# Two chunks' values in one PSUM bank, and fixed places for the exponentials, in a two-layer cross-attention block

## The chip, the cores and the metric

The kernel runs on one core of a Trainium2 chip. The metric is device microseconds of one execution. PE is the matrix engine (TensorE; PEld its weight loads), ACT the ScalarE, DVE the VectorE, POOL the GpSimd, SP the engine whose queue issues nearly all DMAs. SBUF is the on-chip memory that all engines read; PSUM, eight banks of 128 partitions by 512 fp32, is what PE writes to.

## What is computed

Two layers, each a self attention, a cross attention and a gated feed-forward part, with layer norms and residuals, for a batch of 4, 512 tokens of width 320, 20 heads of 16, and a context of 1601 rows of width 192:

```python
def _attn(x, ctx, wq, wk, wv, wo, bo, heads):
    q = (x @ wq).reshape(b, n, heads, dh).transpose(0, 2, 1, 3)
    k = (ctx @ wk).reshape(b, j, heads, dh).transpose(0, 2, 1, 3)
    v = (ctx @ wv).reshape(b, j, heads, dh).transpose(0, 2, 1, 3)
    sim = jnp.einsum('bhid,bhjd->bhij', q, k) * dh ** (-0.5)
    a = jax.nn.softmax(sim, axis=-1)
    out = jnp.einsum('bhij,bhjd->bhid', a, v)
    return out.transpose(0, 2, 1, 3).reshape(b, n, heads * dh) @ wo + bo

h1 = _ln(x, n1_g, n1_b)
x = _attn(h1, h1, q1, k1, v1, o1_w, o1_b, heads) + x
h2 = _ln(x, n2_g, n2_b)
x = _attn(h2, context, q2, k2, v2, o2_w, o2_b, heads) + x
h3 = _ln(x, n3_g, n3_b)
a, g = jnp.split(h3 @ ff_w1 + ff_b1, 2, axis=-1)
x = a * jax.nn.gelu(g, approximate=False) @ ff_w2 + ff_b2 + x
```

## The kernel before

**Units.** The work is a list of units, in order: in each layer 20 self units (4 batch entries by 5 groups of 4 heads), 20 cross units (the same) and 4 ff units (one per batch entry). A unit of attention goes through its keys in chunks of 128: 4 chunks in self, 13 in cross (the last has 65 keys). That makes 2 x 20 x (4 + 13) = 680 chunks, 520 of them in cross.

**A chunk** (`main`, L1083). `score` makes the transposed scores of one head, keys on partitions and 512 queries along the free axis, in a bank `st`: two matmuls of the query's high and low parts (`product`, L1096) and one that subtracts the row's maximum (`less_maximum`, L1099). Four heads use the four groups of 32 rows of the PE array, two heads at a time; beside them, in the other two row groups, run the matmuls `sps` (L911) for the maxima of the next unit, which DVE reduces (L932). Then ACT takes the exponential of each `st` into an SBUF tile `pr` (L1109). `values` (L1116) multiplies the values with the four `pr` of a chunk: for each head a matmul to 32 of the 128 partitions of a bank `av` (L1123; two instructions each, so eight a chunk). It is issued one chunk late: `late` collects it and `flush` issues it after the next chunk's scores. The first chunk's `av` is copied to a tile `u.o` (L1134); every further one is copied by ACT to a tile `vo` (L1139) and added to `u.o` by POOL (L1140). In the last cross unit of a layer (`last`) DVE adds the bank to `u.o` instead (L1136), and two of the four `st` lie in `ps_m`.

**The banks.** `ps_st` (L94) has four PSUM banks. The four `st` of a chunk, its `av`, and one bank for most other steps (`step_bank`, L312) are allocated from it, in program order; an allocation waits for the bank that was allocated four before it to be read out. `ps_m` (L95) has two buffers of two banks, for `sps`. The long steps for the context's keys and values (`keys_of_context` L756, `values_of_context` L846) take two banks of `ps_st` and one buffer of `ps_m` (`quarter_banks`, L815).

**The SBUF tiles.** `prs` (L92) is a pool of eight tiles of 128 by 512 fp32, for `pr`, `vo`, and in ff the gate's `gl` and half of the hidden activations `hid` (L1244). `wq1`, `wk1`, `wv1` (L135) hold the self attention's weights, loaded by `load_self` (L191): nine DMAs of rows and six small ones for the norm. `w1` and `w1r` hold the ff weights; in the self and cross stages parts of them hold the cross attention's weights and the context.

**The planner.** Norms, projections (`qps` L702 for queries, `kps` L734 and L764 for keys, `vps` L836 and L854 for values), the output projection (`ops` L1035) and the divisions are steps in chains, each with a cost and a due time counted in rounds, two rounds a chunk. After the `flush` of each chunk `steps` (L372) issues those that are due by a running credit. All of it is decided when the program is built; engines then run their instructions in that order. Steps for the values of a coming unit may only be issued once the unit that uses the place has its values for that chunk (`u.valued`). DMAs of weights wait in a list `loads`; one is issued per chunk, and all that is left at the start of each ff unit (L1439). SP issues DMAs in order.

Of the kernel before, what the change touches and what calls it, by code (L numbers as in the profile page):

```python
# [9 lines left out]
F32 = mybir.dt.float32  # L10
# [7 lines left out]
B, N, D = 4, 512, 320  # L18
S2, CTX = 1601, 192
H, DH = 20, 16  # L20
FF = 4 * D
L = 2
EPS = 1e-5
P = 128
NQ = N // P
G, HG = 5, 4
GD = HG * DH
SLOT = 32
GT = GD // SLOT

VW = DH + 1
# [6 lines left out]
KB = CTX // 32  # L38
# [26 lines left out]
def kernel(ctx: ExitStack, tc: tile.TileContext, x, context, ws, out):  # L65
# [18 lines left out]
    nc = tc.nc  # L84
    dma = nc.sync.dma_start

    const = ctx.enter_context(tc.tile_pool(name="const", bufs=1))
    wpool = ctx.enter_context(tc.tile_pool(name="weights", bufs=1))
    one = ctx.enter_context(tc.tile_pool(name="one", bufs=1))
    two = ctx.enter_context(tc.tile_pool(name="two", bufs=2))  # L90
    three = ctx.enter_context(tc.tile_pool(name="three", bufs=3))
    prs = ctx.enter_context(tc.tile_pool(name="prs", bufs=8))  # L92
    dram = ctx.enter_context(tc.tile_pool(name="dram", bufs=1, space=bass.MemoryType.DRAM))
    ps_st = ctx.enter_context(tc.tile_pool(name="ps_st", bufs=4, space=PSUM))  # L94
    ps_m = ctx.enter_context(tc.tile_pool(name="ps_m", bufs=2, space=PSUM))  # L95
# [6 lines left out]
    columns_of = const.tile([P, NC2 * H * VW + SLOT - VW], F32, name="vals")  # L102
# [29 lines left out]
        return [lambda t=t: part(t) for t in range(NQ)]  # L132


    wq1, wk1, wv1 = (wpool.tile([P, 3, D], F32, name=n) for n in ("wq1", "wk1", "wv1"))  # L135
    wo = wpool.tile([P, 3, D], F32, name="wo")
    w1 = wpool.tile([P, 2, 2 * FF], F32, name="w1")

    w1_flat = w1.rearrange("p k f -> p (k f)")
# [5 lines left out]
    w1r = wpool.tile([P, FF], F32, name="w1r")  # L145
# [4 lines left out]
    wq2 = w2_flat[:, : 3 * D].rearrange("p (k d) -> p k d", d=D)  # L150
    kw = 4 * (HALF + 32)
    kstage = [w2_flat[:, 3 * D + i * kw : 3 * D + (i + 1) * kw].rearrange("p (a w) -> p a w", a=4) for i in range(2)]
    b1 = wpool.tile([P, 2 * NHC], F32, name="b1")

    brow = [wpool.tile([P, D], F32, name=f"brow{i}") for i in range(2)]
# [5 lines left out]
    loads = deque()  # L161
# [29 lines left out]
    def load_self(l):  # L191
        return [lambda: load_norm(l, 0)] + [
            f for t, n in ((wq1, "q1"), (wk1, "k1"), (wv1, "v1")) for f in load_rows(t, ws[l][n], DK)
        ]
# [70 lines left out]
    units = []  # L265
# [44 lines left out]
    start = {"on": True, "both": False}  # L310
# [87 lines left out]
    def until(test, name):  # L398
        while not test():
            assert chains[name], name  # L400
            run(name)
# [113 lines left out]
    def load_context(b, i):  # L515
        c0, n = CGRP[i]
        t = ctx_room[i % 2]
        rows = min(S2, (c0 + n) * P) - c0 * P
        full = rows // P
        if full:  # L520
            dma(
                out=t[:, :full, :],
                in_=context[b, c0 * P : (c0 + full) * P, :].rearrange("(c p) d -> p c d", p=P),
            )
        if rows % P:
            nc.vector.memset(t[rows % P // SLOT * SLOT :, full, :], 0.0)
            dma(out=t[: rows % P, full, :], in_=context[b, (c0 + full) * P : S2, :])
        ctx_in[b, i] = t, clock["round"]
# [537 lines left out]
    late = []  # L1066
# [16 lines left out]
    def main(u, give, nxt):  # L1083

        pr = {}

        def score(c, j, st=None):
            r = min(P, u.nkeys - c * P)
            rows = slice(j * SLOT, (j + 1) * SLOT)
            if st is None:  # L1090
                st = ps_st.tile([P, N], F32, tag="st", name="st")
            keys = u.kT[rows, u.k0 + u.cols[c] : u.k0 + u.cols[c] + r].bitcast(F32R)
            two_rows = slice(j * SLOT, j * SLOT + 2)

            def product(e):
                nc.tensor.matmul(st[:r, :], lhsT=keys, rhs=u.q[rows, e, :].bitcast(F32R), start=(e == 0), stop=False)  # L1096

            def less_maximum():
                nc.tensor.matmul(  # L1099
                    st[:r, :],  # L1100
                    lhsT=units_of[two_rows, :r].bitcast(F32R),
                    rhs=u.mrow[two_rows, :].bitcast(F32R),
                    start=False,
                    stop=True,
                )

            def exponential():
                p = prs.tile([P, N], F32, tag="pr", name="pr")
                nc.scalar.activation(p[:r], st[:r], AF.Exp)  # L1109
                pr[c, j] = p  # L1110

            return [lambda: product(0), lambda: product(1), less_maximum], exponential

        last = nxt is None or nxt.kind == "ff"

        def values(c):  # L1116
            r = min(P, u.nkeys - c * P)
            if u.g in (0, 2):
                until(lambda: units[u.i - u.g].vmade[u.g // 2] > c, "values")
            ps = ps_st.tile([P, N], F32, tag="st", name="av")  # L1120
            for j in range(HG):
                head = (c * H + u.g * HG + j) * VW
                nc.tensor.matmul(  # L1123
                    ps[j * SLOT : (j + 1) * SLOT, :],
                    lhsT=columns_of[:r, head : head + SLOT],
                    rhs=pr.pop((c, j))[:r, :],
                    start=True,
                    stop=True,
                )
            u.valued = c + 1  # L1130

            if c == 0:
                u.o = three.tile([P, N], F32, tag="o", name="o")
                (nc.vector.tensor_copy if last else nc.scalar.copy)(u.o, ps)  # L1134
            elif last:
                nc.vector.tensor_tensor(u.o, ps, u.o, ALU.add)  # L1136
            else:
                vo = prs.tile([P, N], F32, tag="pr", name="vo")
                nc.scalar.copy(vo, ps)  # L1139
                nc.gpsimd.tensor_tensor(u.o, u.o, vo, ALU.add)  # L1140
            if c == u.nch - 1:
                add_finish(u)

        for c in range(u.nch):
            extra = []
            if last:

                both = ps_m.tile([P, 2, N], F32, tag="m", name="st")
                round_of([lambda j=j: score(c, j, both[:, j % 2] if j > 1 else None) for j in range(HG)], [])
                tick()  # L1150
            else:
                for odd in range(2):
                    if odd:
                        tick()
                    pair, rounds = give(2 * c + odd)
                    extra += rounds
                    round_of([lambda j=j: score(c, j) for j in ((2, 3) if odd else (0, 1))], pair)
            u.scored = c + 1

            start["both"] = True  # L1160
            if extra:
                round_of([], extra[0])
            start["both"] = False
            flush()
            late.append(lambda c=c: values(c))
            steps(None, 1 if extra or c == u.nch - 1 else 2)
            for i, e in enumerate(extra[1:]):
                if i and next_cost() is not None:
                    run(pick())
                start["both"] = True  # L1170
                round_of([], e)
                start["both"] = False
            if not last and c == u.nch - 3:
                max_reduce(nxt)
                max_end(nxt)
            if loads:
                loads.popleft()()
# [21 lines left out]
    def ff_main(u, give, nxt):  # L1199
# [42 lines left out]
                    )  # L1242

        def gate(c, pss):  # L1244
            gl = prs.tile([P, N], F32, tag="pr", name="gl")
            nc.scalar.activation(gl, pss[1], AF.Gelu, bias=b1[:, NHC + c : NHC + c + 1])  # L1246
            if c >= len(hid):
                hid.append(prs.tile([P, N], F32, tag="pr", name="hid"))
            nc.vector.scalar_tensor_tensor(hid[c], pss[0], b1[:, c : c + 1], gl, ALU.add, ALU.mult)  # L1249

        def banks():
# [43 lines left out]
    def before(u):  # L1295

        if u.kind == "cross" and u.g == 1 and u.b + 1 < B or u.kind == "self" and u.m == EARLY - 2:
            b = u.b + 1 if u.cross else 0
            if u.l == 0:
                load_context(b, 0)  # L1300
                load_context(b, 1)
        if u.kind == "cross" and u.m == B * G - 1:
            loads.extend(load_first(u.l))
        if u.kind == "self" and u.m == EARLY:

            add_context(u.l, 0, lambda s: units[u.i - u.m + B * G].own.update(kv=s["cT"], tail=s["tail"]), u.start + 36, yes)

    def after(u):

        stage[u.b] += 1  # L1310
        if u.b == B - 1:
            load_bias(u.l, ("self", "cross", "ff").index(u.kind) + 2)
            if u.kind == "self":
                loads.extend(load_out(u.l, "o2_w"))
            if u.kind == "cross" and u.l + 1 < L:
                loads.extend(load_out(u.l + 1, "o1_w"))
            if u.l + 1 < L:
                if u.kind == "ff":
                    loads.extend(load_cross(u.l + 1))
                    loads.extend(load_ff(u.l + 1))  # L1320
                elif u.kind == "self":
                    loads.extend(load_self(u.l + 1))

    def left(v):
        return sum(map(len, v.pairs))
# [152 lines left out]
```

## Time and profile before

| what | value |
| --- | --- |
| median of 3 runs | 3263.91 us (3244.82 to 3268.62) |
| profiled execution, time | 3260.33 us |
| profiled execution, span | 3258.5 us |
| mean granted clock of PE | 0.965 of full |
| exponentials `pr` (L1109), ACT | 2720, 603 ns each |
| copies `vo` (L1139), ACT | 576, 606 ns each |
| adds `o` (L1140), POOL | 576, 1284 ns each |
| values `av` (L1123), PE | 5440 instructions, 765.4 us busy in all |
| maxima `pm` (L932), DVE | 980, 1194 ns each |

In the stages, the self attention of layer 0 ends and its cross attention begins at 456 us of the span; the cross attention goes to about 1368, the ff to about 1666, the second layer's self attention to 2065 and its cross attention to about 2978. The page gives busy times per engine, the chain of work that ended last, and groups of instructions by line. Busy times of PE are of pipelined matmuls whose ends are modelled, so that a short wait can lie inside a busy stretch. The list of waits names, for each engine and line, what ended an idle time: microseconds in total, how often, and the longest. The timeline gives instructions in order of time: start and length in us, engine, line, operation, what is written from what, and in brackets the idle time before. `PEld` is a weight load, and a bank that a matmul must wait for is waited for by its weight load already.

### The profile page before, as it was taken

Reading aid. Unit: us, or ns where it says so; the run is one execution under the profiler, and the core shown is the slowest. Engines: PE = TensorE matmul, PEld = TensorE weight load, DVE = VectorE, ACT = ScalarE, POOL = GpSimd, SP = SyncE. Lnnn points to the kernel's source line nnn. Section 1 sums busy time; section 2 is a strip of 40 time slices with the busy share of each in tenths; the row PEclk is TensorE's granted clock in tenths of the full one; section 3 lists DMA queues with packets and bytes.
Section 4 is the critical chain, followed back from the end, with each engine's and each line's share of the span. In section 5 each row is a group of like instructions: output and inputs, shape, how many; then the busy total and the mean of one; then the engine's idle time right before and its main releaser. Section 6 shows DMA issues by size and latency. Waiting matters only on the chain.

```text
span 3258.5 us, 87733 instructions
## 1 busy us (share of the span) xinstructions
PE 3075.1 (94%) x36690; PEld 1632.1 (50%) x36690; DVE 2097.2 (64%) x2845; ACT 1961.6 (60%) x3949; POOL 1263.3 (39%) x1369
## 2 busy tenths in 40 slices
PE   7899899999999999999998998999999999999999
PEld 3455455455455455455444554554554555544555
DVE  6766777777777777622256777777777777774221
ACT  2666556787777777711136664677777778776110
POOL 2435334554544544211114453345445445442000
PEclk7999889999999999999999998999999999999999
DMA  3333212211211211200113231212121111112000
GB/s 91 86 68 79 44 37 53 66 38 39 54 39 40 63 31 36 69 1 5 26 32 74 66 65 38 43 41 53 33 50 39 36 41 39 40 22 65 9 11 14
DMA packets 213029, 145.00 MB, mean 44 GB/s; under 512 B 65556, under 2 KB 203160, under 8 KB 212632
## 3 DMA queue, kind: packets, MB, share of 16 engines
q1 hardware_dynamic: 211368, 138.32, 19.1%
q8 instruction: 289, 4.73, 0.6%
q10 hardware_dynamic: 1264, 1.06, 0.1%
q14 instruction: 108, 0.88, 0.1%
HBM read 33.04 MB, written 7.93 MB: 13 GB/s over the span
## 4 chain that ended last, share of the span: by engine, by line
PE 69%; DVE 11%; POOL 5%; ACT 4%; issue 4%; SPq 3%; DMA 3%; ACTq 0%; DVEq 0%; POOLq 0%
PE av L1123 16%; PE st L1096 14%; PE fps L1223 9%; PE yps L1279 5%; PE st L1099 5%; DVE pm L932 4%; PE sps L911 4%; ACT pr L1109 4%; PE kps L764 3%; PE vps L854 3%; PE qps L702 3%; PE ops L1035 3%; PE fps L1236 2%; DVE nmax L932 2%; SPq L991 2%
## 5 line engine op out<-in xcount | busy, mean ns | idle before, releaser
L1109 ACT ACTIVATE pr<-st 128x512 f32<-128x512 f32 (+1 forms) x2720 | 1414.0, 603 | 422.0 <-PE st L1099 362.9
L932 DVE TENSOR_REDUCE pm<-sps 128x2 f32<-128x1024 f32 (+1 forms) x980 | 1132.8, 1194 | 197.6 <-PE sps L911 155.8
L1140 POOL TENSOR_TENSOR o<-o,vo 128x512 f32<-128x512 f32 x576 | 739.8, 1284 | 1194.8 <-ACT vo L1139 1145.4
L1096 PE MATMUL st<-q,kT 32*128 32x512 f32 (+1 forms) x5440 | 1021.2, 444 | 50.6 <-ACT pr L1109 19.2
L911 PE MATMUL sps<-kT,q 32*128 32x512 f32 (+1 forms) x6400 | 988.7, 410 | 55.2 <-DMA kT<-stage 24.0
L1123 PE MATMUL av<-pr,vals 128*32 128x512 f32 (+1 forms) x5440 | 765.4, 630 | 35.5 <-ACT pr L1109 32.8
L1096 PEld LDWEIGHTS st<-q,kT 32*128 32x128 f32 (+1 forms) x5440 | 505.0, 183 | 517.3 <-ACT pr L1109 283.1
L1099 PE MATMUL st<-m,units 2*128 2x512 f32 (+1 forms) x2720 | 620.4, 401 | 20.0 <-DMA m<-turned 18.0
L911 PEld LDWEIGHTS sps<-kT,q 32*128 32x128 f32 x6400 | 478.7, 188 | 105.6 <-DVE pm L932 33.7
L932 DVE TENSOR_REDUCE nmax<-sps 128x2 f32<-128x1024 f32 (+1 forms) x356 | 381.3, 1110 | 174.8 <-PE sps L911 120.1
L1139 ACT COPY vo<-av 128x512 f32<-128x512 f32 x576 | 348.8, 606 | 52.5 <-PE av L1123 50.2
L1099 PEld LDWEIGHTS st<-m,units 2*128 2x128 f32 (+1 forms) x2720 | 317.3, 184 | 67.2 <-issue 27.1
L1223 PE MATMUL fps<-hT,w 128*128 128x512 f32 x640 | 284.6, 597 | 1.8 <-DVE hid L1249 1.8
L1246 ACT ACTIVATE gl<-fps,b 128x512 f32<-128x512 f32 x80 | 50.6, 684 | 369.7 <-PE fps L1236 268.1
L1123 PEld LDWEIGHTS av<-pr,vals 128*32 128x32 f32 (+1 forms) x5440 | 111.7, 109 | 303.9 <-ACT pr L1109 282.1
L1249 DVE SCALAR_TENSOR_TENSOR hid<-fps,b,gl 128x512 f32<-128x512 f32 x80 | 56.4, 747 | 252.5 <-ACT gl L1246 252.5
L1223 PEld LDWEIGHTS fps<-hT,w 128*128 128x128 f32 x640 | 118.6, 190 | 151.2 <-issue 145.9
L609 POOL TENSOR_SCALAR stage<-stage 128x256 fp32r<-128x256 f32 (+1 forms) x155 | 107.2, 692 | 183.9 <-ACT stage L710 97.8
L1279 PE MATMUL yps<-w,hid 128*128 128x320 f32 x640 | 175.4, 434 | 0.0
L1279 PEld LDWEIGHTS yps<-w,hid 128*128 128x128 f32 x640 | 120.6, 190 | 55.8 <-issue 7.0
L609 POOL TENSOR_SCALAR w<-w 128x896 fp32r<-128x896 f32 x40 | 98.1, 2452 | 109.1 <-DVE w L774 109.1
L1035 PEld LDWEIGHTS ops<-wo,aT 112*32 112x32 f32 (+1 forms) x3072 | 100.5, 113 | 67.4 <-issue 34.0
(82 smaller groups left out, 2310.5 us busy)
## 6 DMA issues: line engine op xcount, KB each, us to landing
kT<-w SPq DMA_DIRECT2D x160, 192.0 KB
q<-stage SPq DMA_DIRECT2D x320, 64.0 KB
q<-stage SPq DMA_DIRECT2D x154, 128.0 KB
aT<-o SPq DMA_DIRECT2D x320, 32.0 KB
m<-turned SPq DMA_DIRECT2D x636, 2.0 KB
kT<-stage SPq DMA_DIRECT2D x156, 64.0 KB
w<-in_L_xattn_ff_w_dram SPq DMA_DIRECT2D x20, 256.0 KB
ctxT<-ctxT SPq DMA_DIRECT2D x24, 208.0 KB
```

The lines of the kernel that those rows point to most:

```text
L609: eng.tensor_scalar(high.bitcast(F32R), x, 1.0, None, ALU.mult)
L911: nc.tensor.matmul(out, lhsT=u.q[rows, e, queries].bitcast(F32R), rhs=u.kT[rows, keys].bitcast(F32R), start=(e == 0), stop=(e == 1),)
L932: nc.vector.tensor_reduce(to[:, j : j + n], part, AX.X, ALU.max, negate=(ns == 1))
L1035: nc.tensor.matmul(ps[f : f + m, : D // 2], lhsT=aT[:n, k, t * P + f : t * P + f + m], rhs=wo[:n, k, cols], start=(k == 0), stop=(k == 2),)
L1096: nc.tensor.matmul(st[:r, :], lhsT=keys, rhs=u.q[rows, e, :].bitcast(F32R), start=(e == 0), stop=False)
L1099: nc.tensor.matmul(st[:r, :], lhsT=units_of[two_rows, :r].bitcast(F32R), rhs=u.mrow[two_rows, :].bitcast(F32R), start=False, stop=True,)
L1109: nc.scalar.activation(p[:r], st[:r], AF.Exp)
L1123: nc.tensor.matmul(ps[j * SLOT : (j + 1) * SLOT, :], lhsT=columns_of[:r, head : head + SLOT], rhs=pr.pop((c, j))[:r, :], start=True, stop= ...
L1139: nc.scalar.copy(vo, ps)
L1140: nc.gpsimd.tensor_tensor(u.o, u.o, vo, ALU.add)
L1223: nc.tensor.matmul(ps, lhsT=w1[:, k, i * FF + c * P : i * FF + (c + 1) * P], rhs=u.hT[:, k, :], start=ahead and k == 0, stop=not ahead and ...
L1279: nc.tensor.matmul(ps[:, :D], lhsT=hid[c][:, t * P : (t + 1) * P], rhs=w2[:, c, :], start=(c == 0), stop=(c == NHC - 1),)
```

## The change

Three things are changed together. In cross units `values` takes a list of two chunks: the matmuls of both go to one bank, the first chunk's with `start`, the second's with `stop`, so that PE adds them up; then one copy and one add follow for the two. It is issued one chunk after the second, so in the program even chunks (2, 4, ... 12) are followed by 16 value instructions and odd ones by none; the thirteenth chunk stands alone and is issued in the next unit's first chunk. Self units go on with one chunk at a time.

The pool `prs` is replaced by a fixed tile `own` of eight places, and `place()` goes round them in turn: in self units ten places (two more in unused columns of `w1` and `w1r`), in cross units thirteen (five more in the self attention's weights, which become one tile `wself`). The ff part uses the eight places by number.

Because cross now writes to the self attention's weights, `load_self` for the next layer is put into `loads` at the first ff unit, and no longer at the end of the self stage.

```diff
-    prs = ctx.enter_context(tc.tile_pool(name="prs", bufs=8))
...
-    wq1, wk1, wv1 = (wpool.tile([P, 3, D], F32, name=n) for n in ("wq1", "wk1", "wv1"))
+    wself = wpool.tile([P, 9 * D], F32, name="wself")
+    wq1, wk1, wv1 = (wself[:, i * 3 * D : (i + 1) * 3 * D].rearrange("p (k d) -> p k d", d=D) for i in range(3))
...
+    own = const.tile([P, 8, N], F32, name="pr")
+    mine = [own[:, i, :] for i in range(8)]
+    places = {
+        "self": mine + [w1_flat[:, (2 * KB + 2) * D : (2 * KB + 2) * D + N], w1r[:, 4 * CTX : 4 * CTX + N]],
+        "cross": mine + [wself[:, i * N : (i + 1) * N] for i in range(5)],
+    }
+    at_place = {"kind": "self", "i": -1}
+
+    def place():
+        these = places[at_place["kind"]]
+        at_place["i"] = (at_place["i"] + 1) % len(these)
+        return these[at_place["i"]]
...
+        if at_place["kind"] != u.kind:
+            at_place.update(kind=u.kind, i=min(at_place["i"], len(mine) - 1))
...
-                p = prs.tile([P, N], F32, tag="pr", name="pr")
+                p = place()
...
-        def values(c):
-            r = min(P, u.nkeys - c * P)
+        def values(cs):
             if u.g in (0, 2):
-                until(lambda: units[u.i - u.g].vmade[u.g // 2] > c, "values")
+                until(lambda: units[u.i - u.g].vmade[u.g // 2] > cs[-1], "values")
             ps = ps_st.tile([P, N], F32, tag="st", name="av")
-            for j in range(HG):
-                head = (c * H + u.g * HG + j) * VW
-                nc.tensor.matmul(
-                    ps[j * SLOT : (j + 1) * SLOT, :],
-                    lhsT=columns_of[:r, head : head + SLOT],
-                    rhs=pr.pop((c, j))[:r, :],
-                    start=True,
-                    stop=True,
-                )
-            u.valued = c + 1
-
-            if c == 0:
+            for c in cs:
+                r = min(P, u.nkeys - c * P)
+                for j in range(HG):
+                    head = (c * H + u.g * HG + j) * VW
+                    nc.tensor.matmul(
+                        ps[j * SLOT : (j + 1) * SLOT, :],
+                        lhsT=columns_of[:r, head : head + SLOT],
+                        rhs=pr.pop((c, j))[:r, :],
+                        start=(c == cs[0]),
+                        stop=(c == cs[-1]),
+                    )
+            u.valued = cs[-1] + 1
+
+            if cs[0] == 0:
...
-                vo = prs.tile([P, N], F32, tag="pr", name="vo")
+                vo = place()
...
-            if c == u.nch - 1:
+            if u.valued == u.nch:
                 add_finish(u)
+
+
+        n = 2 if u.cross else 1
+        together = {min(c + n, u.nch) - 1: list(range(c, min(c + n, u.nch))) for c in range(0, u.nch, n)}
...
-            late.append(lambda c=c: values(c))
+            if c in together:
+                late.append(lambda cs=together[c]: values(cs))
...
-            gl = prs.tile([P, N], F32, tag="pr", name="gl")
+            gl = mine[5 + c % 3]
...
-                hid.append(prs.tile([P, N], F32, tag="pr", name="hid"))
+                hid.append(mine[c - 5])
...
+        if u.kind == "ff" and u.b == 0 and u.l + 1 < L:
+            loads.extend(load_self(u.l + 1))
...
-                elif u.kind == "self":
-                    loads.extend(load_self(u.l + 1))
```

## The prediction

> **What bounds the kernel now.** I read the page first, for the busy shares and the chain that ended last.
>
> ```profile
> PE 3075.1 (94%) x36690; PEld 1632.1 (50%) x36690; DVE 2097.2 (64%) x2845; ACT 1961.6 (60%) x3949; POOL 1263.3 (39%) x1369
> ...
> PE 69%; DVE 11%; POOL 5%; ACT 4%; issue 4%; SPq 3%; DMA 3%; ACTq 0%; DVEq 0%; POOLq 0%
> ```
>
> PE carries the chain; ACT and POOL, which the change relieves, hold 4% and 5% of it. So ACT or POOL time that goes is worth only what PE waits for. The list of waits, longest first, says where that is.
>
> ```profile
> ACT pr L1109 <- PE st L1099: 362.9, 517, 11.7
> ...
> PEld st L1096 <- ACT pr L1109: 283.1, 349, 1.7
> PEld av L1123 <- ACT pr L1109: 282.1, 610, 0.7
> ...
> ACT pr L1109 <- POOL o L1140: 37.3, 27, 1.6
> ```
>
> `PEld av <- ACT pr` is no wait for data, since the values read exponentials a chunk old. It is the wait for a PSUM bank: the four banks of `ps_st` hold a chunk's four `st`, and the next allocation, `av`, needs the first of them back from its exponential. 610 of 680 chunks have it. Next, the timeline of two neighbouring cross chunks (start, length):
>
> ```profile
> 1315.99 0.16 PEld L1123 LDWEIGHTS av<-pr,vals 128*32 128x32 f32 x8 [0.37 <-ACT pr L1109]
> 1316.00 1.06 PE L1123 MATMUL av<-pr,vals 128*32 128x512 f32 x8
> ...
> 1316.99 0.50 PE L1096 MATMUL st<-q,kT 32*128 32x512 f32 x2
> ...
> 1317.25 0.62 ACT L1139 COPY vo<-av 128x512 f32<-128x512 f32 x1
> ...
> 1317.56 0.40 PE L1099 MATMUL st<-m,units 2*128 2x512 f32 x1
> ...
> 1317.92 0.18 PEld L1096 LDWEIGHTS st<-q,kT 32*128 32x128 f32 x1 [0.30 <-ACT vo L1139]
> ...
> 1317.99 2.06 ACT L1109 ACTIVATE pr<-st 128x512 f32<-128x512 f32 x4
> ...
> 1318.49 0.39 PE L1099 MATMUL st<-m,units 2*128 2x512 f32 x1
> ...
> 1318.81 0.16 PEld L1123 LDWEIGHTS av<-pr,vals 128*32 128x32 f32 x8 [0.35 <-ACT pr L1109]
> 1318.81 1.07 PE L1123 MATMUL av<-pr,vals 128*32 128x512 f32 x8
> ```
>
> This is the loop that matters. A chunk's scores start; 1.00 us later its first exponential starts (1316.99 to 1317.99), 0.60 us long, the others each 0.49 behind ((2.06-0.60)/3). Only when the first ends can `av` start, which takes PE 1.0. Those 1.0 us are what PE does while ACT empties banks. Chunks with nothing else between values and the next scores (I call them unfilled) take 2.7 to 2.8 us. Others hold a step of the planner (`qps`, `ops`, `kps`, `vps`), a filler, there.
>
> Last, windows over a cross stage (length; PE, PEld, DVE, ACT, POOL busy; clock; DMA):
>
> ```profile
> 500.00:1300.00 800.00, 763.19 (x10888) 412.38 (x10878) 606.99 (x739) 609.46 (x1245) 391.75 (x359) 0.98 0.21 46
> ```
>
> No engine is full; the loop's latency holds PE.
>
> **The change part by part.** The cross stages run from 456 to 1368 and 2065 to 2978 us, 56% of the span.
>
> *Copies and adds.* 38 units lose 6 `vo` copies and 6 adds each: 228 x 0.606 = 138 us of ACT, 228 x 1.284 = 293 us of POOL. On the path, by itself: nothing, as PE waits for banks and not for these engines' shares. Matmuls stay as many; accumulating into one bank has no row here, between -1 and +1 us over 240 pairs if an accumulating column runs as the two score passes into one `st` do; I take 0.
>
> *Values together.* Odd chunks now have no `av`, even ones 2.0 us of it. `av`'s bank wait does not vanish: whatever PE does next needs the first bank back just as much. I work an unfilled odd chunk with its even neighbour, t = 0 at the odd chunk's first score, 0.07 from a bank's release to PE. Exponentials end at 1.60, 2.09, 2.58, 3.06. The even chunk's first score goes at 1.67, its second at 2.16 (in-order PE holds the passes behind it), second pass +0.33, maximum's pass +0.23 at 2.72; exponential +0.43 at 3.15, ending 3.75. Its third `st` goes at 2.95, its fourth at 3.13, last maximum 3.69, values at 4.0, end 6.0. Before, such a pair took 5.54 (median of the 52 pairs with both unfilled). So +0.46 a pair. Ordering PE's matmuls by start, I counted 114 unfilled odd chunks among the 228 of the 38 units: +52 us. The price lies between 0 (the 16-matmul run lets ACT catch up fully) and 0.8 (if a DVE step of 0.3 also falls between the maxima's reductions, which with two `ps_m` buffers have no slack there).
>
> *Filled odd chunks.* The filler now starts behind the scores, at 1.67, where `av` had covered it until 2.7. `kps` and `vps` fillers (18 + 21) need two `ps_st` banks and a `ps_m` one: the latter waits for the reduction of the odd chunk's first maxima (0.75 to 2.0), so 2.07 instead of 1.67: +0.4 x 39 = 16. A `qps` (35) ends at 2.3, but its copy on ACT stands behind the exponentials until 3.06 + 0.28, and the next chunk's fourth score needs that bank: 0.25 x 35 = 9. An `ops` (28) is read by DVE, about +0.1 each, 2. Other way: scores-to-values is 1.82 us after an unfilled and 1.66 after a filled chunk; after a double `av` it is 1.66 always, for the 57 filled odd ones behind unfilled even chunks -9. Together +18 (between -9 and +40).
>
> *Exponentials' places.* Before, eight `prs` buffers serve nine live tiles, so a chunk's fourth exponential takes the buffer of `vo` from the POOL add: the 27 waits above, all in cross, when POOL is busy with `kps`'s split (2.45 and 2.11 us). Of them 17 of 1.57 us fall before an unfilled boundary and show in the next chunk (3.4 to 3.9 us from scores to values against 1.8); the other ten cost about 0.3: 17 x 1.57 + 10 x 0.3 = 30 us of PE. With 13 places and a `vo` every second chunk the reused place was last read two or more chunks ago, so all 30 go. What is late next is the exponential's own ring above. Self has 10 places; no wait of this kind shows there: 0.
>
> *The last cross unit of each layer* uses `ps_m` for two scores and DVE for the sums: 12 fewer DVE adds, but the same loss of cover: +4 (between -4 and +8).
>
> *Self weights later.* Nine weight DMAs and six small ones leave layer 0's cross and are issued at its first ff unit, waiting on SP for the last values, which the ff's flush has put ahead on PE. An issue costs SP about 0.52 us (the chain's `SPq L991` pieces), so 8 us of queue; behind it stand the four `aT` of the last cross unit, whose projection is due rounds later. PE is 100% busy in 1400 to 1600, so 0; without that cover, 8 us plus 1.26 MB at the 85 GB/s of the first 100 us, 23 us once.
>
> *ff gates in fixed places:* the same eight tiles, 0.
>
> Sum: 52 + 18 - 30 + 4 = +44 us. Against the profiled execution (span 3258.5, time 3260.3) 3304; the median of the runs is 3.6 higher, so 3308.
>
> One rule is weighed. The row: with 610 bank waits the cross stage's granted clock is 0.98, the ff's 1.00, the self's, with 7 us DMA waits, 0.90 to 0.94; so waits under 1 us cost the clock little, and I add nothing.
> The Trainium skill, "TensorE: Matmul & The Clock Gate", section on the second HAM failure mode, says that cycling through PSUM banks with short idles between matmul groups can make the clock fall to half and recover again and again. By its window of about 3.4 us, one such window per unfilled pair would be 1.7 x 114 = 194 us more, an estimate from that page.
>
> **The rivals.**
>
> *Cover is enough (faster).* Place: the unfilled odd chunk. If ACT, freed of a copy there, runs far enough ahead that the double `av` absorbs its backlog, the price per pair falls to 0 and the filled ones' to -9: 3264 - 9 - 30 = 3225. It decides from 0.26 us a pair downward if the filled ones cost nothing (30/114), 0.1 if they cost 18. For: 0.49 us of ACT a pair is freed, and ACT waits 363 us for `st`. Against: four banks allow ACT no lead over PE. At the far end, with both limits gone, a pair is 9 x 0.49 = 4.4 of ACT or 2 x 1.27 + 2.0 = 4.5 of PE, 1.0 less: 3264 - 114 - 30 = 3120.
>
> *Ring loss and place gain cancel:* 0.26 x 114 = 30: 3264.
>
> *Places are followed as one tile (much slower).* If a write to one place orders against reads of all eight, `av` would wait for its chunk's last exponential, 1.46 us after the first: 280 groups x 1.46, 3264 + 410 = 3670. Against: `kT` and `vals` are written in parts beside reads and show no such wait.
>
> **How the numbers follow.** A change under 1% (33 us) cannot be told here. Forecast, net +15 to +100 us (pair price 0.3 to 0.8): 0.67, of which 0.54 lies beyond +33. Cancelling: 0.12. Faster rival: 0.18, of which 0.16 beyond -33. One tile: 0.03. So slower 0.57, same 0.27, faster 0.16. Range: the low end is the faster rival's 3225, beyond which lies about 0.13; the high end is 3264 + 91 + 40 - 30 = 3365 with the pair at 0.8, beyond it 0.06.
>
> **What would show it.** Right: `vo` x348 with ACT down 138 us; no wait of `pr` for POOL; `PEld av <- ACT pr` in fewer, but `PEld st <- ACT pr` and those of the fillers in more times; unfilled odd-even pairs at 6.0; cross stages longer by some 20 us each, self and ff as before. Wrong: unfilled pairs at or under 5.5, or PE matmuls waiting for `pr`'s last exponential.

## The result, and the profile after

The changed kernel takes 3267.22 us in the median of 20 runs (3261.48 to 3280.86), the kernel before 3258.64 (20 runs): a ratio of 1.0032, 95% interval 1.0018 to 1.0046. It is slower by about 10 us, a third of a per cent, where the forecast was 44 us. (The forecast's 3308 stood on a median of 3 runs, 3263.91; with 20 runs the kernel before lies 5 us lower.)

The page after, its first row and the chain:

```profile
PE 3117.7 (95%) x36690; PEld 1686.7 (52%) x36690; DVE 2077.9 (64%) x2833; ACT 1866.6 (57%) x3721; POOL 972.6 (30%) x1141
...
PE 80%; DVE 8%; ACT 4%; issue 3%; DMA 2%; SPq 2%; POOL 1%; ACTq 0%; DVEq 0%; POOLq 0%
```

ACT has 228 instructions and 95 us less, POOL 228 and 291 us less, and the kernel is no faster for it. (138 us were forecast for ACT; 95 is 0.42 us a copy. ACT's instructions overlap: four exponentials of 0.60 us take 2.06 us in the timeline before.) PE took over POOL's and DVE's parts of the chain. The timeline of one unfilled odd chunk and its even neighbour (times from the span's start, lengths, in brackets the idle time before and its releaser):

```profile
1307.29 0.50 PE L1113 MATMUL st<-q,kT 32*128 32x512 f32 x2
...
1309.00 0.18 PEld L1113 LDWEIGHTS st<-q,kT 32*128 32x128 f32 x1 [0.24 <-ACT pr L1126]
...
1309.48 0.18 PEld L1113 LDWEIGHTS st<-q,kT 32*128 32x128 f32 x1 [0.31 <-ACT pr L1126]
...
1310.46 0.18 PEld L1113 LDWEIGHTS st<-q,kT 32*128 32x128 f32 x1 [0.31 <-ACT pr L1126]
...
1311.35 0.11 PEld L1141 LDWEIGHTS av<-wself,vals 128*32 128x32 f32 x1 [0.37 <-ACT wself L1126]
...
1313.21 0.49 PE L1113 MATMUL st<-q,kT 32*128 32x512 f32 x2
```

The ring of four banks is there as it was worked out by hand: the even chunk's first, second and fourth score start 1.71, 2.19 and 3.17 us after the odd chunk's first (by hand 1.67, 2.16, 3.13), each behind an exponential; the values start at 4.06 (4.0). Only the end differs: the double run of values takes 1.85, not 2.0, so the pair is over at 5.92 and not 6.0. Over all 52 pairs of two unfilled chunks the median is 5.93, against 5.54 before.

The waits after (microseconds in total, times, longest):

```profile
PEld st L1113 <- ACT pr L1126: 160.2, 329, 1.7
...
PEld av L1141 <- ACT pr L1126: 133.3, 286, 0.9
...
PEld st L1113 <- ACT wself L1126: 88.6, 182, 0.8
...
PEld av L1141 <- ACT wself L1126: 44.1, 106, 0.7
...
ACT pr L1126 <- POOL o L1158: 2.7, 2, 1.4
```

The exponentials' wait for POOL is gone but for 2 of 27. The bank wait of `av` fell from 282.1 to 177.4 us (both kinds of place together), that of `st` from 283.1 to 248.8; counted in times, `av` fell from 610 to 392 and `st` rose from 349 to 511.

The planner put the same fillers at the same chunks, 114 unfilled odd ones in both kernels, so the 38 units (the last cross unit of each layer apart) can be compared class by class. The times between starts of PE's matmuls, summed, in us:

| 38 cross units | before | after | places alone |
| --- | --- | --- | --- |
| 114 pairs, odd chunk unfilled | 772.8 | 803.5 | 729.1 |
| 114 pairs, odd chunk filled | 831.2 | 834.3 | 831.6 |
| 38 first chunks of a unit | 161.3 | 136.3 | 171.6 |
| sum | 1765.3 | 1774.1 | 1732.3 |

The third column is the first experiment below. Self, ff and the last cross units changed by under 6 us each.

### The profile page after: what moved, and what is told of

The parts are those of the page before. It is cut to its first block, busy times and chain, and to the rows that moved or that the text cites. A ratio compares the mean times of both kernels' runs of the same rounds, so it can differ in the third digit from the quotient of the medians.

```text
span 3265.6 us, 89144 instructions
## 1 busy us (share of the span) xinstructions
PE 3117.7 (95%) x36690; PEld 1686.7 (52%) x36690; DVE 2077.9 (64%) x2833; ACT 1866.6 (57%) x3721; POOL 972.6 (30%) x1141
## 4 chain that ended last, share of the span: by engine, by line
PE 80%; DVE 8%; ACT 4%; issue 3%; DMA 2%; SPq 2%; POOL 1%; ACTq 0%; DVEq 0%; POOLq 0%
PE av L1141 19%; PE st L1113 19%; PE fps L1246 9%; PE st L1116 6%; PE yps L1302 5%; PE sps L926 5%; DVE pm L947 3%; PE kps L779 3%; PE qps L717 3%; PE vps L869 3%; PE ops L1050 3%; DVE nmax L947 2%; PE fps L1259 2%; ACT pr L1126 2%; PE kps L749 1%
## 5 line engine op out<-in xcount | busy, mean ns | idle before, releaser
L1113 PE MATMUL st<-q,kT 32*128 32x512 f32 (+1 forms) x5440 | 1089.3, 445 | 40.5 <-DVE x L1057 8.0
L1126 ACT ACTIVATE pr<-st 128x512 f32<-128x512 f32 (+1 forms) x1791 | 947.1, 602 | 269.9 <-PE st L1116 252.1
L1141 PE MATMUL av<-pr,vals 128*32 128x512 f32 (+1 forms) x3582 | 644.5, 636 | 16.9 <-ACT pr L1126 10.3
L1158 POOL TENSOR_TENSOR o<-o,pr 128x512 f32<-128x512 f32 x236 | 302.2, 1281 | 951.2 <-ACT pr L1157 931.2
L1126 ACT ACTIVATE wself<-st 128x512 f32<-128x512 f32 (+1 forms) x801 | 427.6, 602 | 75.1 <-PE st L1116 68.6
L1141 PE MATMUL av<-wself,vals 128*32 128x512 f32 (+1 forms) x1602 | 344.5, 635 | 3.6 <-ACT pr L1126 3.0
L1269 ACT ACTIVATE pr<-fps,b 128x512 f32<-128x512 f32 x80 | 50.6, 683 | 370.4 <-PE fps L1259 268.1
L1158 POOL TENSOR_TENSOR o<-o,wself 128x512 f32<-128x512 f32 x89 | 114.0, 1281 | 381.5 <-ACT wself L1157 381.5
L1157 ACT COPY pr<-av 128x512 f32<-128x512 f32 x236 | 140.9, 597 | 135.7 <-PE av L1141 134.7
L1050 PE MATMUL ops<-wo,aT 112*32 112x160 f32 (+1 forms) x3072 | 128.5, 303 | 4.1 <-ACT pr L1126 2.8
```

The source lines that it names most:

```text
L1050: nc.tensor.matmul(ps[f : f + m, : D // 2], lhsT=aT[:n, k, t * P + f : t * P + f + m], rhs=wo[:n, k, cols], start=(k == 0), stop=(k == 2),)
L1141: nc.tensor.matmul(ps[j * SLOT : (j + 1) * SLOT, :], lhsT=columns_of[:r, head : head + SLOT], rhs=pr.pop((c, j))[:r, :], start=(c == cs[0] ...
```

## The experiments

All ratios are to the kernel before, which was run again beside each set of experiments (medians 3259.40 to 3261.07). The theory after the first look: the pairing costs about 60 us where nothing covers the ring; the places give 30; some 25 come back at units' ends, where PE had waited for the maxima's row `m`.

**1. The places without the pairing.**

```diff
-        n = 2 if u.cross else 1
-        together = {min(c + n, u.nch) - 1: list(range(c, min(c + n, u.nch))) for c in range(0, u.nch, n)}
+        together = {c: [c] for c in range(u.nch)}
```

> Every chunk's values are issued alone again; the thirteen and ten fixed places and the later load of the self weights stay. Theory (the pairing costs about 60 us in unfilled odd chunks and gives about 25 back where a unit's maxima arrive; the places give 30): the 27 waits of exponentials for POOL are gone, everything else is as before, so 3229 us, ratio 0.991 to before, and the waits for m<-turned stay at some 18 to 24 us. Rival (the waits for POOL were hidden from PE, the places are worth nothing and the whole change is near 0 by itself): 3259, ratio 1.000.

Measured: 3227.81 us, 0.9903 (0.9881 to 0.9924). The theory's 3229 holds. The places make the kernel 1% faster (the later load of the self weights comes with them; the self and ff stages moved by less than 3 us); pairing on top of them costs 39 us (3267.22 against 3227.81). By the table: +74 in unfilled pairs, +3 in filled ones, -35 in units' first chunks. PE's waits for `m` did not go with the places alone:

```profile
PE st L1116 <- DMA m<-turned: 18.1, 19, 1.5
...
PEld st L1116 <- DMA m<-turned: 6.1, 5, 1.6
```

**2. The pairing moved by one chunk**, so that the stretch between a unit's last maxima and the next unit's first subtraction holds one double run instead of two.

```diff
-        n = 2 if u.cross else 1
-        together = {min(c + n, u.nch) - 1: list(range(c, min(c + n, u.nch))) for c in range(0, u.nch, n)}
+        first, n = (1, 2) if u.cross else (0, 1)
+        groups = [[0]] * first + [list(range(c, min(c + n, u.nch))) for c in range(first, u.nch, n)]
+        together = {cs[-1]: cs for cs in groups}
```

> The pairing is moved by one chunk: chunk 0 alone, then 1 with 2, up to 11 with 12, so that even chunks have no values and the last pair is issued in the next unit's first chunk. As many copies, adds and pairs as in the changed kernel. Theory (m<-turned no longer holds PE because a double values run now lies behind chunk 10 and another behind chunk 12, between the last maxima and the next unit's first subtraction): with the shift that stretch holds one double run less, some 8.5 us instead of 10.7, the waits for m<-turned come back with 18 us or more, and the time is 20 to 40 us over the changed kernel: 3285 to 3305, ratio 1.008 to 1.014. Rival (m comes earlier because DVE, POOL and SP have less to do): the waits stay gone and the time is that of the changed kernel, 3267.

Measured: 3285.57 us, 1.0087 (1.0067 to 1.0107), 18 us over the changed kernel. PE's waits for `m`, in the list of waits of the kernel before:

```profile
PE st L1099 <- DMA m<-turned: 18.0, 19, 1.5
...
PEld st L1099 <- DMA m<-turned: 6.0, 7, 1.5
```

The same in the list of the changed kernel:

```profile
PEld st L1116 <- DMA m<-turned: 3.9, 5, 1.6
...
PE st L1116 <- DMA m<-turned: 1.7, 3, 1.2
```

And in that of the kernel with the pairing moved:

```profile
PE st L1116 <- DMA m<-turned: 14.4, 15, 1.4
...
PEld st L1116 <- DMA m<-turned: 7.1, 7, 1.6
```

That is 24.0, 5.6 and 21.5 us. The eight `m` DMAs take SP 4.1 us from the first to the last issue in all three; from the last to the next unit's first score there are 0.85, 2.42 and 0.67 us (medians of 38). So the pairing hid this wait by where its double runs lie, not because SP, DVE or POOL were freer: with the shift they are as free and the wait is back. The time lies at the low edge of what was expected. The 18 us are not the price of this wait alone: the chunks without values are now the even ones, and the half clock (below) holds for 133 us in the 38 units instead of 82.

**3 and 4. The pairing only where the odd chunk is filled, and only where it is unfilled.**

```diff
-        n = 2 if u.cross else 1
-        together = {min(c + n, u.nch) - 1: list(range(c, min(c + n, u.nch))) for c in range(0, u.nch, n)}
+        groups = []
+        for c in range(0, u.nch, 2 if u.cross else 1):
+            two_of = [c, c + 1] if u.cross and c + 1 < u.nch else [c]
+            unfilled = c + 1 in UNFILLED.get(u.i, ())
+            groups += [two_of] if last or not unfilled else [[k] for k in two_of]
+        together = {cs[-1]: cs for cs in groups}
```

`UNFILLED` lists the 114 chunks by unit; the other kernel has `last or unfilled`.

> Two chunks are paired only where the odd chunk holds a filler (114 of 228 pairs); where it is unfilled both are issued alone. Theory (the pairing's price is all in unfilled odd chunks, 0.5 us each): the 58 us are gone, the places' 30 stay and perhaps half of the 25 at the units' ends: 3223 us, between 3211 and 3235, ratio 0.986 to 0.993. Rival (the price lies on every pair alike, half of it stays): 3245 to 3255.

> The other half: paired only where the odd chunk is unfilled. Theory: 58 us lost there, 30 won by the places, about 12 at the units' ends: 3275 us, between 3263 and 3290, ratio 1.001 to 1.010, slower than the kernel with pairs where filled by some 50. Rival (the price lies on every pair alike): as the other half, 3245 to 3255.

Measured: 3232.66 us, 0.9925 (0.9902 to 0.9947), and 3283.03, 1.0070 (1.0046 to 1.0094). The halves differ by 50 us, as expected: the price lies where there is no filler. Against the places alone pairing at filled chunks costs 5 and at unfilled ones 55; both together cost 39. The wait for `m` does not account for that: 24.2 us with the places alone, 13.7 and 13.9 in the two halves and 5.6 with all pairs nearly add up. The half clock does not add up (68, 65, 106 and 82 us in the 38 units), which is part of it by the traces; no run shows the rest.

**5 and 6. Work for the hole.** Three matmuls that nobody reads, behind the scores of each of the 114 chunks, in the changed kernel and in the one with the places alone.

```diff
             flush()
+            if c in UNFILLED.get(u.i, ()):
+                idle = ps_st.tile([P, N], F32, tag="st", name="idle")
+                for _ in range(3):
+                    nc.tensor.matmul(idle[:, :P], lhsT=ident, rhs=units_of, start=True, stop=True)
```

> The changed kernel with three matmuls of 128 columns (some 0.6 us of PE by a guess from the 512-column rows) into a spare bank of ps_st, read by nobody, behind the scores of each of the 114 unfilled odd chunks. Theory (in these chunks PE stands still for about as long, since nothing covers the exponentials' ring): the work falls into the hole, the even chunk's wait for its values shrinks by as much, unfilled pairs stay near 5.93 and the time within 15 us of the changed kernel: 3267 to 3282. Rival (PE is full at 95% busy and the price of pairing is something else than an uncovered wait): 114 x 0.6 = 68 us more, 3335.

> The same three matmuls at the same 114 places in the kernel with the places alone, where each of these chunks has its own values as cover. Theory: little hole is left there (unfilled pairs take 5.55, PE's own work in them about 4.7), so the work is paid for by more than half: 40 to 70 us over 3228, 3268 to 3298. Rival (PE has as much room here as there): 3228 to 3240.

Measured: 3272.16 us, 1.0044 (1.0026 to 1.0062), and 3283.19, 1.0073 (1.0049 to 1.0097). The three matmuls occupy 0.865 us of PE, more than the guess, 99 us in all. With the pairing they cost some 5 us of 99 (the two intervals overlap); where single values cover the ring, 55. In the pair's own parts (median of the 52 with both unfilled) the even chunk's stretch from scores to values shrinks from 2.36 to 1.71 and the pair grows from 5.93 to 6.19, by 0.26 for 0.865; with the places alone it grows from 5.55 to 6.37, by 0.82. The rest of the near-free ride goes with the clock, below. The idle matmuls also take a bank of the ring, so this is not PE work alone, and the profiled execution took 3282.61 us, 10 over the median.

**7. The copies alone.** The places, and in cross every second chunk's `vo` copy and add left out, so that those chunks' values are missing.

```diff
+            elif u.cross and cs[0] % 2:
+                pass
             else:
                 vo = place()
                 nc.scalar.copy(vo, ps)
```

> The places alone, and in cross every second chunk's copy of av by ACT and add by POOL are left out (so these chunks' values are missing from the output); as many copies and adds as in the changed kernel, without its pairing. It measures what the copies are worth by themselves. Theory (as predicted: PE waits for banks, not for ACT's or POOL's share): little, 0 to 20 us under 3228. Rival (ACT's copies hold PE in the unfilled chunks): 0.49 us in each of 114 pairs and more, 55 us or more, 3172 or less.

Measured: 3200.24 us, 0.9808 (0.9781 to 0.9834), 28 us under the places alone: more than my 20, half of the rival's 55. Leaving them out is worth something by itself, 14 us in units' first chunks and 10 in unfilled pairs, whose median stays 5.55. It frees not only ACT and POOL: those `av` banks wait for no copy, and PE's waits for a score's bank behind a copy fall from 71 to 41 us, so which of the two is paid for is open. The pairing's other effects cost 67 us (3267 less 3200), and the relief pays 28 of them.

**8 to 10. The end of the maxima earlier.** If the wait for `m` is worth 20 us, it can be had without pairing:

```diff
+            ready = not last and c == u.nch - 3
+            if ready and len(extra) < 2:
+                max_reduce(nxt)
+                max_end(nxt)
             steps(None, 1 if extra or c == u.nch - 1 else 2)
...
-            if not last and c == u.nch - 3:
+            if ready and len(extra) > 1:
                 max_reduce(nxt)
                 max_end(nxt)
```

> The places alone, and the end of the next unit's maxima (max_reduce and max_end, with their eight m DMAs) is issued before the planner's steps of that chunk, not after them, where all maxima are done by then. Theory (PE waits some 24 us for m<-turned at units' ends because the SP queue and DVE get to it late): part of the 24 us goes, 3205 to 3222. Rival (the eight issues on SP of 4.6 us and the landing set it, not the place in the queues): 3228.

Measured: 3232.6 us, 0.9917 (0.9895 to 0.9940): no gain over the places alone. In the trace the two cross stages are 29 us shorter and the two self stages 34 longer. So the early end was kept for cross units alone (`ready and u.cross and ...`), with the places alone and with the pairing:

> The places alone, with the early end of the maxima in cross units only (in self it cost 34 us, in cross the two stages went down by 30). Theory: the waits for m<-turned fall from 24 us to under 8 and the time is that of the places less 25 to 30: 3198 to 3205, ratio 0.981 to 0.984, the fastest of these kernels. Rival (what cross won, self had only shifted into it): 3228.

> The changed kernel, pairs and all, with the same early end of the maxima in cross units. Theory (the pairing has hidden the wait for m<-turned already; last of the eight issues 2.4 us before the next unit's first score against 0.9): nothing is left to win by it, 3259 to 3270. Rival (the early end wins by something else than that wait, such as DVE's order): 25 to 30 us here too, 3238 to 3243.

Measured: 3195.82 us, 0.9813 (0.9787 to 0.9839), the fastest kernel here, 1.9% under the one before; and 3246.23, 0.9959 (0.9944 to 0.9973). The first is as expected, though 9.1 us of the wait for `m` are left. The second is not: 21 us came off a kernel that hardly waited for `m`. Its trace shows where: the 38 last chunks of a unit (chunk 12) take 172 us instead of 198, and nothing else moves by more than 6 (the half clock in chunk 12 fell with it, from 41 to 14 us). In the changed kernel's timeline, at such a chunk:

```profile
1249.45 0.33 DVE L1057 TENSOR_TENSOR x<-ops,x 128x160 f32<-128x160 f32 x1 [1.59 <-PE ops L1050]
...
1249.93 0.80 DVE L998 TENSOR_SCALAR nm<-nmax 128x16 fp32r<-128x16 f32 x1
...
1251.18 2.31 DVE L947 TENSOR_REDUCE pm<-sps 128x2 f32<-128x1024 f32 x2
...
1252.42 0.79 PE L926 MATMUL sps<-kT,q 32*128 32x512 f32 x2 [0.47 <-DVE pm L947]
```

DVE idles 1.59 us for a filler's `ops`, and only behind it comes to the end of the maxima (`nm` and three more), then late to the next reductions, for which PE's `sps` waits at 1252.42. With the places alone the early end changes chunk 12 by 3 us only. So part of what the pairing wins at units' first chunks it loses again in chunk 12. The rival was half right.

**The clock.** The granted clock is full or half, in windows of 3.41 us. The windows view of the kernel before, for the second layer's cross stage (length; PE, PEld, DVE, ACT, POOL busy; mean clock; DMA share and GB/s):

```profile
2100.00:2900.00 800.00, 763.53 (x10920) 414.37 (x10915) 598.02 (x697) 607.25 (x1237) 390.31 (x358) 0.97 0.19 40
```

The changed kernel, both cross stages:

```profile
500.00:1300.00 800.00, 778.11 (x10753) 432.99 (x10750) 591.57 (x727) 560.00 (x1128) 257.67 (x255) 0.97 0.20 45
2100.00:2900.00 800.00, 782.50 (x11081) 440.26 (x11075) 600.50 (x704) 569.66 (x1146) 262.08 (x259) 0.99 0.19 40
```

The places with the early end in cross:

```profile
500.00:1300.00 800.00, 770.82 (x11098) 417.67 (x11090) 624.57 (x757) 629.30 (x1288) 401.26 (x367) 0.99 0.20 45
2100.00:2900.00 800.00, 776.89 (x11067) 417.15 (x11063) 612.75 (x732) 639.82 (x1308) 404.70 (x383) 0.99 0.20 42
```

The figure behind the five busy times is the clock: 0.97 before in this stage (0.98 in the first layer's), 0.97 and 0.99 after, 0.99 and 0.99 in the last. By the trace's clock records, in the 38 units the half clock holds for 89 us before, 82 after, 68 with the places alone, 27 with the early end. It sits where PE waited: before, 31 us in units' first two chunks (24 of them behind the wait for `m`), and 37 in chunk 4, behind the exponentials' wait for POOL; after, 41 in chunk 12. With the idle work it is 34 instead of 82, worth up to 24 us at half rate, which can account for most of why 99 us of work cost 5. That the layers of the profiled execution went apart (cross +17.5 us in the first, -10.2 in the second) goes the same way: half clock 55 and 27 us, against 38 and 51 before. No run held the clock and changed nothing else, so these shares are read from traces, not shown by an experiment.

What the pairing did to the clock shows by classes (half clock in us, 38 units):

| | before | after | places alone |
| --- | --- | --- | --- |
| unfilled pairs | 47 | 80 | 16 |
| filled pairs | 28 | 0 | 24 |
| first chunks | 14 | 2 | 28 |

All 20 stretches of half clock after begin in the even chunk behind an unfilled odd one, in the hole; with the places alone none of 13 does. No long wait precedes them: in the 3.41 us before each, PE's longest idle is 0.49 us or less. The one of the timeline above, as windows:

```profile
1248.92:1252.34 3.42, 2.76 (x38) 1.39 (x26) 2.72 (x7) 2.32 (x5) 1.29 (x1) 1.00 0.00 0
1252.34:1259.16 6.82, 6.74 (x42) 2.61 (x46) 3.51 (x4) 2.79 (x6) 0.00 (x0) 0.50 0.02 2
```

An estimate: if half of the half-clock time is lost, the pairing without it costs 43 us in unfilled pairs (114 times 0.38, the difference of the medians, is 43 as well), 15 in filled ones and wins 22 in first chunks, and the places win 28 in unfilled pairs. The 20 unfilled pairs with half clock in them agree with the half: they take 8.76 us on average, with 4.0 us of half clock each, and the other 94 take 6.68.

## Why the prediction was wrong

The sum was +44 and the runs gave +10. By its terms, with the profiled executions (+7 us of span):

- **Unfilled odd chunks, +52, and the places, -30: right in kind, both too small.** Undoing one at a time gives +74 for the pairing in these chunks and -44 for the places; together +31 where the forecast had +22. The pair worked out by hand was right to 0.1 us (5.92 for 6.0). What it left out is in the means: without the half clock, by the estimate above, they are +43 and -28, near the forecast.
- **Filled odd chunks, +18: measured +3, of which the clock took some 14** (28 us of half clock before, none after), so about +17 without it. That this is near 18 is partly luck. The step that put an accumulating run at 2.0 us ("I take 0") was wrong: 16 value instructions in one bank take 1.85, two runs of 8 take 2.0, which is 0.15 x 114 = 17 us less in these pairs. Against that, the later `kps` came (2.78 instead of 2.46 us from its first matmul to the next chunk), and pairs with an `ops` were put far too low: 6.43 us before, 7.21 after (medians of 26), where 0.1 was forecast.
- **Units' ends: no term at all, -25 measured in units' first chunks.** This is the step that failed. PE's waits for `m` fell by 18 us (24.0 to 5.6), which is nearly all of the 19 left when the clock is taken off. The list of waits that I read has `PE st <- DMA m<-turned` with 18.0 us. I costed the moved values by what covers the exponentials' ring, and did not ask what else they would come to cover. Chunks 8 and 9 now put their values behind chunk 10's scores and chunks 10 and 11 behind chunk 12's, so that four chunks' values instead of three lie there, and the last of the eight DMAs is issued 2.42 instead of 0.85 us ahead of the next unit's first score. The shift by one chunk brings the wait back. Some of the gain is lost again in chunk 12, where the early end of the maxima is worth 26 us with the pairing and 3 without.
- **The copies and adds, 0 by themselves: too low.** Without the pairing, 228 fewer are worth 28 us, the earlier release of their banks included.
- **Last units, +4, measured -1.7; the later load of the self weights, 0:** self and ff changed by about 5 us or less.
- **"Waits under 1 us cost the clock little":** this step was wrong, and that it cost nothing is luck. The half clock is as long in the net (89 us before, 82 after) only because windows behind POOL and `m` went while the hole brought its own: 80 us in unfilled pairs against 16 with the places alone, up to 32 us of time, behind idles of no more than 0.49 us.
- Most signs named for a right forecast came: 348 `vo`, 2 waits for POOL left of 27, pairs near 6.0, and `PEld st <- ACT pr` more often (349 to 511 times, though shorter in total). ACT fell by 95 us, not 138, the fillers' waits did not become more, and only the first cross stage is longer by the 20 us said. So these signs did not tell this forecast from a change that costs 10 us.

The rule that was weighed, the Trainium skill's "TensorE: Matmul & The Clock Gate" (the second HAM failure mode: short idles between PSUM groups make the clock swing), stood with an estimate of 194 us. The half clock in the cross units is 7 us shorter after the change than before it, so in the net the row was nearer. The kind of thing the rule describes is in the traces all the same, at a smaller size: half-clock windows sit in 20 of the 114 unfilled pairs, behind short idles, and not in all of them. That is up to 32 us against the places alone, where the estimate had 194.

The faster rival, which had the price at 0 in unfilled odd chunks, was wrong there: their pairs rose to 5.93 us. The places, a shorter accumulating run and the units' ends paid for the ring, not ACT's lead.

## What to carry to other kernels

Work that is moved along an in-order engine uncovers one wait and covers another; list every wait of that engine between the old place and the new, not only the one at the old. Halving an evacuation saves little when its product was also the cover for a ring of banks: fill the hole first, or pair where a filler stands. And undo the parts of a bundled change one at a time: here one part was worth 1% and the other took it back. Price short waits with the clock in mind, by where the half clock lies in the trace and not by its mean over a stage.

## What was not expected of the hardware

- Accumulating eight more value instructions in the same bank is cheaper than starting a new run: 1.85 us for 16, 1.00 for each 8 (medians over the 38 units).
- Half-clock windows of 3.41 us follow short idles. By the traces (matmul ends are modelled), before, 16 of the 20 stretches in the 38 units have a PE idle of 1.0 to 1.8 us in the 3.41 us ahead of them; after, none of 20 has one over 0.49 us. What decides it is not shown. The three cheapest kernels here hold the half clock in the 38 units for 27, 41 and 68 us, the three dearest but the idle-work ones for 133, 106 and 82.
- 99 us of added PE work cost some 5 us where it fell into waits and the half clock went from 82 to 34 us, and 55 where there was little room.
